# A graph network's second layer: additions, Relu, one-hots and sums of a group moved next to its first products

## The chip, the cores and the metric

The kernel runs on one core of a Trainium2 chip. A core has five engines that run their own programs and wait for each other by semaphores: TensorE (PE, matrix products, with its weight loads PEld), VectorE (DVE), ScalarE (ACT), GpSimd (POOL) and SyncE (SP), which issues most of the DMAs. [...] The metric is the device time of one execution in microseconds (us).

## The reference

The program has 12500 nodes with 64 features and 212500 edges (two random directions of 100000 pairs and a loop at each node), sorted by target. It has two layers, each behind a layer norm and a Relu. The first multiplies each source row by the weight of its edge's relation (16 of them) and sums by target. The second, which the change touches, is a small network on each edge:

```
h = jnp.maximum(_layernorm(x, axis=-1), 0.0)
msg_input = jnp.concatenate([h[src], h[dst], edge_attr], axis=1)
hid = jax.nn.relu(msg_input @ W1 + b1)
msg = hid @ W2 + b2
x = x + jax.ops.segment_sum(msg, dst, num_segments=12500)
```

All in float32.

## The kernel before, in words

The kernel splits W1 by its rows. The first layer ends by writing, for each node, `a_rows` (its row times the part of W1 for sources) and `b_rows` (its row times the part for targets, with b1). An edge's hidden row is then Relu of its source's `a_rows`, plus its target's `b_rows`, plus its eight attributes times the rest of W1. Loop edges are left to a separate path, so some 200000 edges remain. They stand in tiles of 128, four tiles to a group: 391 groups (`NGC`), in the order of their targets, so that one group's targets lie in a window of at most 40 nodes (`W`).

For each group `second_layer` (from line 1382) does this:

- POOL gathers the sources' rows with four indirect DMAs, one a tile, into a landing buffer `rows` (`gather`, line 966). There are 14 such buffers, so POOL can be 14 groups ahead of the addition that empties them.
- SP loads the window of `b_rows` into one of six `b_win` buffers (line 1417), and once in four groups the edges' places in the window (`local_bc`) and their attributes (`of_edges`, lines 1402 to 1412).
- At every second group ACT makes two groups' one-hots by node, with two activations (`off`, then `of_edges`, lines 1428 and 1429).
- **First products:** PE multiplies them with the window into `pz` (line 1435). A float32 product is two matmuls with two weight loads in the trace, so a group has eight of each. The first four groups have more: two further products a tile, for the last blocks of nodes (lines 1436 to 1443). [...]
- **Addition** `z` (line 1448): DVE adds products and gathered rows.
- **Relu** (line 1454): ACT writes `hid`.
- **One-hots** `oh` (line 1456): DVE compares the edges' places with a row of numbers, 128 edges by 40 nodes.
- **Sums** `pa` (line 1470): PE multiplies `hid` by `oh` and so sums the group's edges into 65 by 40. One PSUM tile holds four groups; there are two such tiles.
- **Table addition** (line 1477): DVE adds the 65 by 40 to a running table, `sums`, at a place that it reads from memory into a register.

Beside this, one step an iteration of `open_step` finishes two blocks of nodes in eight groups: it multiplies finished sums by W2 and stores them, and does the loop edges (`results` and `own_edges`, lines 1355 and 1333, whose products all land in `po`).

What sets the order: each engine's instructions are chained in the order in which the Python loop issues them (`InOrder`, line 322, used as `V_`, `S_`, `T_`, `Q_`, `P_`), so the order that is written is the order of every engine's program. The loop at line 1395 runs over iterations `it`; group `it` has its loads, gathers and first products in it, and the other steps of a group come some iterations later. How many is set by four pairs at line 121 and by `turns` (line 127): with a pair `(most, least)` a group's step comes `most` iterations after its first products, and over the last 40 groups the distance shrinks, one in four groups, to `least`. Within an iteration the order is: first products, `z`, Relu and one-hots, sums, one step of `open_step`, table addition. So at iteration `it` PE makes `pz` of group `it` and `pa` of group `it - 6`, DVE makes `z` of `it - 3`, `oh` of `it - 4` and the table addition of `it - 9`.

What an instruction waits for is worked out by the framework from the tiles it touches. [...]

Of the kernel before, what the change touches and what calls it, by code (L numbers as in the profile page):

```python
# [40 lines left out]
F32 = mybir.dt.float32  # L41
# [9 lines left out]
P = 128  # L51
N = 12500
D = 64
# [15 lines left out]
DA = D + 1  # L69


G = 4
W = 40
# [44 lines left out]


L1_PE, L1_ADD = (2, 1), (4, 2)  # L120
L2_Z, L2_HID, L2_PE, L2_ADD = (3, 1), (4, 1), (6, 1), (9, 1)


BEGIN = 8
# [74 lines left out]
def bc(ap, axis, n, shape):  # L199
    return ap.unsqueeze(axis).to_broadcast(shape)  # L200
# [3 lines left out]
def gnn_kernel(  # L204
# [101 lines left out]
    def in_order():  # L306
        with ExitStack() as c2:
# [858 lines left out]
            def chain(*parts):  # L1166
                for part in parts:
                    yield from part
# [147 lines left out]
            def load_mid(k):  # L1316
                b0, nb = BLOCKS[k]
                mids[k] = wk2.tile([P, BS, D], F32, name="x_r", bufs=3)[:, :nb]
                Q_.dma_start(mids[k], x_mid[b0 * P : (b0 + nb) * P, :].rearrange("(b p) d -> p b d", p=P))
# [62 lines left out]
            def second_layer(ps):  # L1382

                iota_p = ps.tile([P, W], F32, name="iota_p", bufs=1)
                V_.tensor_copy(iota_p, iota_s[:, :W])
                for k in range(2):
                    load_mid(k)
                load_own(0)
                open_step = chain(
                    own_edges(0, sums[0], 0, ps), own_edges(BS, sums[0], AHEAD2, ps), own_edges(2 * BS, sums[1], AHEAD2, ps)  # L1390
                )
                a_of, n_of, oh_of, pz_of, hid_of, pa_of = {}, {}, {}, {}, {}, {}
                at, at_b = {}, {}
                of_z, of_hid, of_pe, of_add = (turns(lag, NGC) for lag in (L2_Z, L2_HID, L2_PE, L2_ADD))
                for it in range(NGC + L2_ADD[1]):

                    g = it
                    if g < NGC:
                        if g % RG == 0:
                            at_b.update(enumerate(windows(first_row, g, PAD_DST, Q_, min(RG, NGC - g)), g))  # L1400
                        if g % RB == 0:
                            ng = min(RB, NGC - g)
                            local_bc = wk2.tile([W, RB * G * P], BF16, name="local_bc", bufs=3)
                            Q_.dma_start(
                                local_bc[:, : ng * G * P],
                                dst_l[g : g + ng, :].rearrange("g e -> (g e)").unsqueeze(0).to_broadcast([W, ng * G * P]),
                            )
                            of_edges = wk2.tile([WE, RB * G * P], F32, name="of_edges", bufs=3)
                            Q_.dma_start(
                                of_edges[W:, : ng * G * P].rearrange("c (t e) -> c t e", e=P),  # L1410
                                turned_c[g * G * EA : (g + ng) * G * EA, :].rearrange("(t c) e -> c t e", c=EA),
                            )
                        a_of[g], n_of[g] = gather((a_early if g < EARLY else a_rows)[:, :], src_c, g, NTC)
                        n = n_of[g]
                        if n:
                            bw = b_win[g % NBW]
                            Q_.dma_start(bw[:W, :], b_rows[bass.ds(at_b.pop(g), W), :])
                            if g == 1:
                                for _ in range(2, EARLY):
                                    t = wk2.tile([P, 2, G * P], F32, name="of_last", bufs=EARLY - 2)  # L1420
                                    of_last.append([t[:, k] for k in range(2)])
                                for _ in sources_of_last(range(2, EARLY), wk2):
                                    pass
                            if g % 2 == 0:
                                np_ = min(2, NGC - g)
                                cols = slice(g % RB * G * P, (g % RB + np_) * G * P)
                                off = wk2.tile([W, 2 * G * P], BF16, name="off")[:, : np_ * G * P]
                                S_.activation(off, local_bc[:, cols], AF.Abs, bias=neg_w)
                                S_.activation(of_edges[:W, cols], off, AF.Relu, bias=1.0, scale=-1.0)
                                pz = ps.tile([P, 2, G, D], F32, name="pz", bufs=4)  # L1430
                            pz_of[g] = pz[:, g % 2]
                            for i in range(n):
                                k = (g % RB * G + i) * P
                                more = range(2 if g < EARLY else 0)
                                T_.matmul(pz_of[g][:, i, :], lhsT=of_edges[:, k : k + P], rhs=bw, start=True, stop=not more)
                                for b in more:
                                    T_.matmul(
                                        pz_of[g][:, i, :],
                                        lhsT=of_last[g][b][:, i * P : (i + 1) * P],
                                        rhs=a_last[:, b, :],  # L1440
                                        start=False,
                                        stop=(b == 1),
                                    )
                    for g in of_z.get(it, []):
                        n = n_of[g]
                        if n:
                            hid_of[g] = wk2.tile([P, G, D], F32, name="z", bufs=3)
                            V_.tensor_tensor(hid_of[g][:, :n, :], pz_of.pop(g)[:, :n, :], a_of.pop(g)[:, :n, :], op=ALU.add)
                    for g in of_hid.get(it, []):
                        n = n_of[g]  # L1450
                        if n:
                            z = hid_of[g]
                            hid_of[g] = hid[g % NHID]
                            S_.activation(hid_of[g][:, :n, :D], z[:, :n, :], AF.Relu)
                            oh_of[g] = wk2.tile([P, G, W], F32, name="oh", bufs=5)
                            V_.tensor_tensor(
                                oh_of[g][:, :n, :],
                                bc(local[:, g * G : g * G + n], 2, W, [P, n, W]),
                                bc(iota_p, 1, n, [P, n, W]),
                                op=ALU.is_equal,  # L1460
                            )
                    for g in of_pe.get(it, []):
                        n = n_of[g]
                        if n:
                            if g % 4 == 0:
                                pa = ps.tile([DA, 4, W], F32, name="pa", bufs=2)
                            pa_of[g] = pa[:, g % 4, :]
                            r, o = hid_of.pop(g), oh_of.pop(g)
                            for i in range(n):
                                T_.matmul(pa_of[g], lhsT=r[:, i, :], rhs=o[:, i, :], start=(i == 0), stop=(i == n - 1))  # L1470
                    next(open_step, None)
                    for g in of_add.get(it, []):
                        if n_of[g]:
                            if g % RG == 0:
                                at.update(enumerate(windows(place_row, g, SN + AHEAD2 - W, V_, min(RG, NGC - g)), g))
                            to = sums[STEP[g] % 2][:, bass.ds(at.pop(g), W)]
                            V_.tensor_tensor(to, to, pa_of.pop(g), op=ALU.add)
                        if g in FIN:
                            k = FIN.index(g)
                            for _ in open_step:  # L1480
                                pass
                            if k + 1 < NFIN:
                                n = BLOCKS[k][1] * P
                                V_.tensor_copy(sums[(k + 1) % 2][:, :AHEAD2], sums[k % 2][:, n : n + AHEAD2])
                            open_step = results(k, ps)
                for _ in open_step:
                    pass
# [28 lines left out]
            with tc.tile_pool(name="own_ps2", bufs=1, space=PSUM) as psB:  # L1516
                second_layer(psB)
# [464 lines left out]
```

## Time and profile before

| | us |
|---|---|
| median of three runs | 4862.96 (4859.89 to 4871.01) |
| the profiled execution | 4867.39 |
| its span, first to last instruction | 4865.5 |
| gathers of the second layer | from 2493.4 to the end of the last at 4806 |
| POOL busy, of the span | 2988.6 (61%) |
| PE busy, of the span | 2402.1 (49%) |
| ACT busy | 1615.3 (33%) |
| DVE busy | 1408.1 (29%) |

The profile is one execution, taken by the hardware. A line of a group of instructions names engine, operation, the tile written and those read, their shapes, how often, the busy time, the mean time of one in ns, and then the idle time of the engine just before them with what ended most of it. `issue` means that the engine waited for nothing that the profile shows; `remote` that a wait ended by something that the trace doesn't tie to an instruction. A line of the timeline has the start, the duration, the engine, the instruction, and in brackets the idle time before it. Every instruction here is put down to line 331, the helper through which all are issued, so tiles tell them apart: `pz<-b_win,of_edges` are the first products, `pa<-oh,hid` the sums, `sums<-sums,pa` the table addition. (`pa<-oh_r,rows` and `rows<-h_rows` belong to the first layer.)

### The profile page before, as it was taken

What the parts mean: (1) busy time and instruction counts of PE and PEld (TensorE: products, weight loads), DVE (VectorE), ACT (ScalarE), POOL (GpSimd) and SP (SyncE); (2) the same over time, 40 slices, a digit from 0 to 9 for tenths busy, and PEclk for the clock granted to TensorE, in tenths of its full rate; (3) what the DMA queues carried; (4) which work ended last, traced back from release to release, by engine and by line L of the source; (5) the groups of instructions that cost most, each with busy time, mean ns of one, the idle gap of its engine ahead of it and who ended that gap; (6) DMA issues with size and microseconds to landing.
All of it is one profiled execution on the core that took longest, in us unless ns stands there. A gap on an engine that the chain in (4) does not pass through costs nothing.

```text
span 4865.5 us, 51339 instructions
## 1 busy us (share of the span) xinstructions
PE 2402.1 (49%) x14955; PEld 1987.2 (41%) x14955; DVE 1408.1 (29%) x4923; ACT 1615.3 (33%) x3341; POOL 2988.6 (61%) x3169
## 2 busy tenths in 40 slices
PE   0244434444344444444445565665565656565556
PEld 0123323333233333333335455555555545555456
DVE  5566726355122332322221111111111111111112
ACT  3434434444344444444432222222222222222222
POOL 5366656665566666666655666666666666666663
PEclk9755555555565555555555555555555555555555
DMA  3314231353433311111111111111111111121111
GB/s 96 72 37 83 54 67 39 67 82 58 69 52 55 60 40 38 39 36 35 36 41 35 41 38 40 40 41 40 39 41 39 43 37 42 39 42 39 39 39 28
DMA packets 533688, 230.44 MB, mean 47 GB/s; under 512 B 430834, under 2 KB 472880, under 8 KB 532374
## 3 DMA queue, kind: packets, MB, share of 16 engines
q0 software_dynamic: 101152, 111.42, 12.0%
q1 hardware_dynamic: 418949, 112.45, 11.4%
q10 hardware_dynamic: 13298, 3.20, 0.3%
q8 instruction: 122, 2.00, 0.2%
q14 instruction: 167, 1.37, 0.1%
HBM read 191.53 MB, written 35.25 MB: 47 GB/s over the span
## 4 chain that ended last, share of the span: by engine, by line
PE 20%; another core or an unknown queue 20%; issue 20%; ACT 5%; DVE 3%; POOL 2%; DMA 0%; DVEq 0%; SPq 0%; ACTq 0%; POOLq 0%
PE pz L331 10%; PE pa L331 7%; POOL rows L331 2%; ACT off_r L331 2%; PE po L331 2%; ACT oh_r L331 1%; PE pT L331 1%; DVE table L331 1%; DVE z L331 1%; PE hT L331 1%; ACT off L331 0%; DVE sums L331 0%; DVE oh L331 0%; SPq L331 0%
## 5 line engine op out<-in xcount | busy, mean ns | idle before, releaser
L331 POOL DMA_INDIRECT rows<-h_rows,src_c x1533 | 1458.5, 951 | 875.6 <-issue 400.7
L331 POOL DMA_INDIRECT rows<-a_rows,src_c x1547 | 1463.3, 946 | 830.5 <-issue 425.0
L331 PE MATMUL pz<-b_win,of_edges 48*128 48x64 f32 x3126 | 794.3, 410 | 482.2 <-issue 442.5
L331 PE MATMUL pa<-oh_r,rows 128*64 128x96 f32 x6132 | 705.5, 353 | 603.9 <-issue 412.2
L331 PEld LDWEIGHTS pz<-b_win,of_edges 48*128 48x128 f32 x3126 | 719.7, 320 | 546.5 <-issue 476.4
L331 PEld LDWEIGHTS pa<-oh_r,rows 128*64 128x64 f32 x6132 | 532.9, 208 | 778.6 <-issue 674.6
L331 DVE TENSOR_TENSOR table<-table,pa 128x96 f32 x1565 | 393.9, 252 | 984.8 <-remote 651.0
L331 PE MATMUL pa<-oh,hid 128*65 128x40 f32 x3126 | 468.1, 305 | 337.2 <-issue 317.9
L331 ACT ACTIVATE hid<-z 128x256 f32<-128x256 f32 x391 | 153.4, 405 | 1286.3 <-DVE z L331 1021.3
L331 ACT ACTIVATE off_r<-iota_s,code 128x192 bf16<-128x192 f32 x1535 | 569.3, 443 | 0.0
L331 PEld LDWEIGHTS pa<-oh,hid 128*65 128x65 f32 x3126 | 394.3, 221 | 400.9 <-issue 342.0
L331 ACT ACTIVATE oh_r<-off_r 128x768 f32<-128x768 bf16 x392 | 330.2, 842 | 361.2 <-remote 238.2
L331 DVE TENSOR_TENSOR sums<-sums,pa 65x40 f32 x391 | 73.0, 187 | 1114.2 <-remote 776.0
L331 DVE TENSOR_TENSOR z<-pz,rows 128x256 f32<-128x256 f32 x391 | 163.9, 420 | 312.7 <-issue 248.2
L331 PE MATMUL pT<-table,wrel 128*64 128x256 f32 (+1 forms) x800 | 209.6, 566 | 38.2 <-issue 30.7
L331 ACT ACTIVATE off<-local_bc,neg_w 40x1024 bf16<-40x1024 bf16 x196 | 222.2, 1134 | 17.4 <-DVE z L331 10.7
L331 DVE SCALAR_TENSOR_TENSOR table<-b_rel,rsel,hT 128x256 f32<-128x256 f32 (+1 forms) x400 | 170.5, 468 | 169.2 <-remote 109.0
L331 ACT ACTIVATE of_edges<-off 40x1024 f32<-40x1024 bf16 x196 | 206.7, 1054 | 6.2
L331 PE MATMUL hT<-ident,u_in 128*128 128x128 f32 (+3 forms) x107 | 46.8, 438 | 307.7 <-issue 125.8
L331 DVE COPY_PREDICATED k_a<-move,k_a 128x1712 int32<-128x1712 int32 (+8 forms) x124 | 185.6, 1498 | 2.1 <-DVE move L331 0.2
L331 ACT ACTIVATE hid_l<-o_ab 128x128 f32<-128x128 f32 x49 | 15.1, 308 | 475.9 <-DVE o_ab L331 421.1
L331 PEld LDWEIGHTS hT<-ident,u_in 128*128 128x128 f32 (+3 forms) x107 | 18.3, 171 | 340.8 <-issue 181.1
(242 smaller groups left out, 1614.3 us busy)
## 6 DMA issues: line engine op xcount, KB each, us to landing
rows<-a_rows,src_c POOLq DMA_INDIRECT x1547
rows<-h_rows,src_c POOLq DMA_INDIRECT x1533
local_bc<-dst_l SPq DMA_DIRECT2D x97, 160.0 KB
k_a<-in_attr_k SPq DMA_DIRECT2D x8, 1368.0 KB
k_a<-in_attr SPq DMA_DIRECT2D x4, 1716.0 KB
b_win<-b_rows SPq DMA_DIRECT2D x391, 10.0 KB
u_in<-attr_c SPq DMA_DIRECT2D x97, 64.0 KB
turned_c<-u_out SPq DMA_DIRECT2D x97, 64.0 KB
```

The source lines that it names most:

```text
L331: last_ins[self.engine] = getattr(self.engine, name)(*args, **kw)
```

## The change

```
-L2_Z, L2_HID, L2_PE, L2_ADD = (3, 1), (4, 1), (6, 1), (9, 1)
+L2_Z, L2_HID, L2_PE, L2_ADD = (0, 0), (0, 0), (0, 0), (6, 1)
...
-                                pz = ps.tile([P, 2, G, D], F32, name="pz", bufs=4)
+                                pz = ps.tile([P, 2, G, D], F32, name="pz", bufs=3)
...
-                                pa = ps.tile([DA, 4, W], F32, name="pa", bufs=2)
+                                pa = ps.tile([DA, 4, W], F32, name="pa", bufs=3)
```

At iteration `it` PE now makes `pz` and then `pa` of the same group, DVE makes its `z` and `oh`, ACT its Relu, and the table addition is that of group `it - 6` (nearer at the end). Between `pz` and `pa` of a group nothing else stands in PE's program; the steps of `open_step` follow `pa`. ACT's two activations for a pair of groups stand ahead of the first one's Relu and behind the Relu of the group before. `pz` has three PSUM tiles instead of four, `pa` three instead of two. No instruction is added or left out.

## The prediction

> **What bounds the kernel now.** I read the page's slices and groups first, then the waits in the middle of the second layer (3000 to 4800 us), then the timeline around its pauses and its two ends. The change touches the second layer alone: its gathers run from 2493 us, the last steady ones to 4806, and the span ends at 4865.5. [...]
>
> ```profile
> L331 POOL DMA_INDIRECT rows<-a_rows,src_c x1547 | 1463.3, 946 | 830.5 <-issue 425.0
> L331 PE MATMUL pz<-b_win,of_edges 48*128 48x64 f32 x3126 | 794.3, 410 | 482.2 <-issue 442.5
> L331 PE MATMUL pa<-oh,hid 128*65 128x40 f32 x3126 | 468.1, 305 | 337.2 <-issue 317.9
> ```
>
> The waits of that stretch (engine and tile, what it waited for, us, times, longest):
>
> ```profile
> DVE sums L331 <- remote: 626.2, 37, 20.1
> PE pz L331 <- issue: 347.2, 310, 3.7
> POOL rows L331 <- DVE oh L331: 282.2, 70, 6.4
> ```
>
> DVE stands for up to 20 us at a time, PE loses time with nothing shown that it waits for, and POOL is stopped 70 times. The timeline of one such round (start, duration, engine, instruction, idle time before it):
>
> ```profile
> 3637.48 0.19 DVE L331 TENSOR_TENSOR sums<-sums,pa 65x40 f32 x1 [19.96 <-remote]
> ...
> 3638.38 0.94 POOL L331 DMA_INDIRECT rows<-a_rows,src_c  x1 [3.78 <-DVE oh L331]
> ...
> 3657.13 0.94 POOL L331 DMA_INDIRECT rows<-a_rows,src_c  x1 [0.30 <-issue]
> ...
> 3659.63 0.23 PE L331 MATMUL pa<-oh,hid 128*65 128x40 f32 x1 [0.96 <-issue]
> ...
> 3661.03 0.99 PE L331 MATMUL pa<-oh,hid 128*65 128x40 f32 x7 [1.17 <-issue]
> 3661.05 0.19 DVE L331 TENSOR_TENSOR sums<-sums,pa 65x40 f32 x1 [19.92 <-remote]
> ...
> 3661.95 0.95 POOL L331 DMA_INDIRECT rows<-a_rows,src_c  x1 [3.88 <-DVE oh L331]
> ```
>
> POOL issues 16 gathers (four groups), one every 1.25 us (0.95 and 0.30 of issue), and stops because the 14 landing buffers are full until DVE adds products to rows. PE creeps from 3651 on, one instruction in about 0.7 us, and is free again at 3661.03; in the same moment DVE gets a signal of products that PE had finished long before. That is 22.65 us after the first of 16 gathers. At the layer's start POOL issues 56 gathers (16 of a_early, 40 more) without a full stop:
>
> ```profile
> L331 POOL DMA_INDIRECT rows<-a_early,src_c x16: 942/946/947, 2493.4 to 2512.1; - x16
> ```
> ```profile
> 2564.12 0.94 POOL L331 DMA_INDIRECT rows<-a_rows,src_c  x1 [0.30 <-issue]
> 2571.98 0.29 DVE L331 TENSOR_TENSOR o_ab<-o_ab,po 128x128 f32<-128x128 f32 x1 [43.61 <-remote]
> ```
>
> There the release comes 78.6 us after the first. So (78.6 - 22.65)/(56 - 16) = **1.40 us a gather**, plus 0.27: while gathers follow each other, PE's signals and its issue are held up, until 1.40 us times their number has passed. That is the bound. In the stretch of waits 1217 gathers make 304 groups in 1800 us, 5.92 us a group; 4 x 1.40 = 5.60 of it is this floor, and 70 rounds of 4.34 groups lose (1800 - 1217 x 1.40)/70 = 1.37 us each between release and next gather, 0.32 a group. [...]
>
> **The change part by part.** Nothing is removed or added: as many products, additions, Relus, one-hots and gathers. What changes is what an engine can do ahead.
>
> *Table additions.* Before, the addition of the first of four groups stood where the fourth's products had just been issued in the same accumulator tile, so DVE waited for those and did four groups in one burst. Now it comes six groups after its products, three after the tile's last; DVE should not stand there at all. The 626 us of that wait go, but only DVE loses them, and it is idle anyway. Worth nothing by itself: what is late next is z.
>
> *z, Relu, one-hots and pa without lag.* Now PE may not start pz of the next group before pa of this one, which needs Relu, which needs z, which needs PE's signal for pz. By starts and ends of rows: pz 1.97, 0.1 to z, z 0.42, 0.1, Relu 0.42, 0.05, pa 1.03 to the next pz. At every second group ACT's off and of_edges (1.17 + 1.06) begin only after the Relu before and so stand in the path, instead of beside PE. A pair takes 2.27 + 1.97 + 0.1 + 0.42 + 0.1 + 0.42 + 0.05 + 1.03 + 1.97 + 0.1 + 0.42 + 0.1 + 0.42 = 9.4, with three sets of po products in eight groups (1.03 each, all behind even groups) 10.1: **5.05 us a group** when no signal is held. That is under the floor of 5.60, so by itself it costs nothing; its cover is the floor. But a signal that is held now stops the chain.
>
> *How many groups a round holds.* Count from the first gather. The z that allowed it ended 0.27 before (3661.68, gather 3661.95). Relu ends at 0.25, pa begins at 0.3, the odd group's pz runs from 1.35 to 3.3. Are signals prompt then? The row of o_ab at 3639.80 answers a po that ended at 3639.76, 1.4 us into its round; of the pz that ended 4.9 us into it, at 3643.25, the trace's record of PE's signals has nothing before 3646.9. So the second z comes at 3.4, POOL gets a second buffer before it stops at 5.0, and goes on. Relu to 4.3, off and of_edges to 6.6, pz of the third group to 8.6: that signal is held until 8 x 1.40 + 0.27 = 11.5. Two groups a round. If a round starts with an odd group, the second pz is later by 2.2, and the round may hold one; the next then starts with an even one. The nearest row is in the last 40 groups, where the old lags shrink to one:
>
> ```profile
> 4781.11 0.95 POOL L331 DMA_INDIRECT rows<-a_rows,src_c  x1 [3.90 <-DVE oh L331]
> ...
> 4789.87 0.95 POOL L331 DMA_INDIRECT rows<-a_rows,src_c  x1 [0.30 <-issue]
> ...
> 4792.71 0.42 DVE L331 TENSOR_TENSOR z<-pz,rows 128x256 f32<-128x256 f32 x1 [2.30 <-issue]
> ...
> 4793.41 0.94 POOL L331 DMA_INDIRECT rows<-a_rows,src_c  x1 [2.59 <-DVE oh L331]
> ```
>
> Eight gathers, a round of 12.3 us, 6.15 a group, with the release 11.6 after the first. The loss a round is then 12.3 - 8 x 1.40 = 1.1; bounds: 0.9 (z alone ahead of the gather) and 2.7 (if PE, whose issue is slow too, has part of pz left at the release). I take 1.1 by this row: 5.60 + 1.1/2 = 6.15, **0.23 more than now, times 377 groups behind the first 14, +87 us**.
>
> How much PE has in store decides between 0.9 and 2.7. The row: in the round of 3638 PE issues some 100 instructions at full pace, to 3651, before it creeps. [...] No row of this profile shows which of the two holds for the new order.
>
> *Head.* The first four groups have 24 products of pz each, some 6.6 us, now in line with z, Relu and pa: from the release at 2572 z of group 4 comes about 10 us later than the rows around 2594 show. **+10.**
>
> *Tail.* When the last gather is released, 14 groups are left, at 5.05: 13 x 5.05 + 8 for the last sums and results = 74. Now it is 4865.5 - 4809.3 = 56, at 8.6 a pair. **+18.**
>
> *Buffers and SP.* pz has three PSUM tiles instead of four, pa three instead of two. A pair's z is done two pairs before its tile is wanted again, an addition five groups before: nothing, while the order holds; at worst a wait that the chain already has. SP loads b_win six groups ahead, waiting for pz of six groups before: some 36 us of cover against about 2 of landing. Were it gone, 2 us a group.
>
> Sum: +87 + 10 + 18 = +115 on the profiled execution's own 4867.4: 4982. It stands 4.4 above the median of the runs shown, so 4980 is forecast, about 2.4% slower.
>
> **The rivals.** *Rounds of one, or pairs with PE late.* Speaking for it: signals at 4.9 us are held already. One group a round: 5.60 + 1.1 = 6.70, +0.78 x 377 + 28 = +322, 5190. Pairs at 6.95: +388 + 28, 5283. *Signals stay prompt (faster).* Place: PE's signal for pz to DVE. The hold-up may come from PE's own run-ahead crowding the same path; a PE in step with DVE and ACT sends less at once. For it: in the round from 4757.51 a z at 4764.86 follows its pz (ended 4764.7) at once, 7 us in. Then rounds never end and POOL runs at the floor: 5.60, -0.32 x 377 + 28 = -93, 4770. It decides if the third z of a round comes before POOL has stopped, some 10 us in. Against it: 37 waits of DVE average 17 us. *The new order makes no other rounds than four* (the change does nothing to the bound): +28 alone, 4895. That the order isn't what it says is unlikely: each engine's instructions are chained in the order in which they are written.
>
> **How the numbers follow.** Pairs 0.48 (own range 4940 to 5070, by losses of 0.9 to 1.6 a round); singles or late pairs 0.26 (5100 to 5290); rounds as now 0.08; prompt signals 0.18. The range must reach into both outer cases: 4800 to 5200. Within 0.2% (10 us, about what a measurement of this kernel can tell from no change) is only the stretch between the prompt case and the others: 0.06. Faster 0.17, slower 0.77.
>
> **What would show it.** POOL's stops grow from 70 to about 150 in the same stretch, in rounds of 8 gathers; DVE waits at z, some 5 to 8 us each, not at sums; ACT's off waits for Relu; the floor of 1.40 holds. I am wrong if gathers run on in long rounds (then faster), if POOL stops after every four (singles), or if PE still runs pz when DVE is released (late pairs).

## The result and the profile after

On the chip of the first profile the changed kernel took 4890.78 us (median of five runs, 4889.72 to 4895.72) where the kernel before took 4862.96 (4859.89 to 4871.01): a ratio of 1.0058, interval 1.0045 to 1.007. It is slower, as forecast, but by 28 us and not by 115. The profiled execution took 4890.74, its span is 4888.9, 23.4 more than before.

The same three groups of the page after:

```profile
L331 POOL DMA_INDIRECT rows<-a_rows,src_c x1547 | 1462.7, 945 | 844.1 <-issue 420.9
L331 PE MATMUL pz<-b_win,of_edges 48*128 48x64 f32 x3126 | 771.1, 424 | 236.7 <-issue 166.3
L331 PE MATMUL pa<-oh,hid 128*65 128x40 f32 x3126 | 429.7, 312 | 795.7 <-ACT hid L331 526.7
```

POOL's row is nearly what it was (844.1 us idle, 830.5 before). PE's idle time has moved from `pz` to `pa`: it now stands at the sums of each group until the Relu of the same group is there. The waits of the middle, 3000 to 4800 us:

```profile
DVE z L331 <- issue: 986.8, 202, 9.2
...
POOL rows L331 <- DVE oh L331: 311.1, 163, 3.1
```

DVE stands at `z` and no longer at `sums`. POOL stops 163 times instead of 70, as foretold, but for 1.9 us each and not 4.0, so that the total is only 29 us more in 1800. A round in the timeline:

```profile
3601.10 0.94 POOL L331 DMA_INDIRECT rows<-a_rows,src_c  x1 [3.01 <-DVE oh L331]
...
3605.46 0.42 DVE L331 TENSOR_TENSOR z<-pz,rows 128x256 f32<-128x256 f32 x1 [4.30 <-issue]
...
3609.15 1.96 PE L331 MATMUL pz<-b_win,of_edges 48*128 48x64 f32 x8 [1.67 <-issue]
3609.90 0.95 POOL L331 DMA_INDIRECT rows<-a_rows,src_c  x1 [0.31 <-issue]
...
3611.21 0.42 DVE L331 TENSOR_TENSOR z<-pz,rows 128x256 f32<-128x256 f32 x1 [4.48 <-issue]
...
3611.90 0.95 POOL L331 DMA_INDIRECT rows<-a_rows,src_c  x1 [1.06 <-DVE z L331]
...
3615.65 0.95 POOL L331 DMA_INDIRECT rows<-a_rows,src_c  x1 [0.30 <-issue]
3618.22 0.42 DVE L331 TENSOR_TENSOR z<-pz,rows 128x256 f32<-128x256 f32 x1 [5.96 <-remote]
...
3618.92 0.95 POOL L331 DMA_INDIRECT rows<-a_rows,src_c  x1 [2.32 <-DVE oh L331]
```

The `z` at 3605.46 follows its `pz` (ended 3605.37) at once, 4.4 us into the round, as foretold. The next `pz` ends at 3611.11, ten us into the round, and I had held its signal until 8 x 1.40 + 0.27 = 11.5 us, which is 3612.6. The `z` came at once, at 3611.21; POOL stood still for only 1.06 us, a gather's worth of that count was still left, and the round went on to twelve gathers. Their 12 x 1.40 end at 3618.2, and there the next `z` stands, to 0.1 us.

For all rounds I count 1.4025 us for each gather, from 0.25 us after the start of the round's first one (close to the prediction's 1.40 and 0.27). A round ends when this count has run off before 0.25 us behind the next gather's start, and its loss is the time between the two. Between 2650 and 4780 us:

| | rounds | groups a round | loss a round, us | loss a group | a group, us |
|---|---|---|---|---|---|
| before | 81 | 4.41 | 1.38 | 0.313 | 5.923 |
| after | 153 | 2.34 | 0.79 | 0.337 | 5.947 |

The rounds are half as long and lose a little over half as much each. Behind the last gather the groups go one after the other:

```profile
4861.48 0.42 DVE L331 TENSOR_TENSOR z<-pz,rows 128x256 f32<-128x256 f32 x1 [2.54 <-PE pz L331]
...
4866.40 0.42 DVE L331 TENSOR_TENSOR z<-pz,rows 128x256 f32<-128x256 f32 x1 [2.65 <-PE pz L331]
...
4871.51 0.42 DVE L331 TENSOR_TENSOR z<-pz,rows 128x256 f32<-128x256 f32 x1 [2.85 <-PE pz L331]
```

That is 5.0 us a group. By parts, in the two profiled executions: the second layer starts 3.0 us earlier, the first 100 gathers take 3.1 more, the other 1463 take 9.9 more, and behind the last gather there are 73.0 us instead of 59.6, 13.4 more: together +23.4.

### The profile page after: what moved, and what is told of

It reads as the page before. It is cut to its first block, busy times and chain, and to the rows that moved or that the text cites. A ratio compares the mean times of both kernels' runs of the same rounds, so it can differ in the third digit from the quotient of the medians.

```text
span 4888.9 us, 51576 instructions
## 1 busy us (share of the span) xinstructions
PE 2364.0 (48%) x14955; PEld 1941.0 (40%) x14955; DVE 1417.0 (29%) x4923; ACT 1640.1 (34%) x3341; POOL 2988.4 (61%) x3169
## 5 line engine op out<-in xcount | busy, mean ns | idle before, releaser
L331 POOL DMA_INDIRECT rows<-a_rows,src_c x1547 | 1462.7, 945 | 844.1 <-issue 420.9
L331 PE MATMUL pz<-b_win,of_edges 48*128 48x64 f32 x3126 | 771.1, 424 | 236.7 <-issue 166.3
L331 PE MATMUL pa<-oh,hid 128*65 128x40 f32 x3126 | 429.7, 312 | 795.7 <-ACT hid L331 526.7
L331 PEld LDWEIGHTS pz<-b_win,of_edges 48*128 48x128 f32 x3126 | 695.7, 324 | 298.0 <-issue 202.8
L331 PEld LDWEIGHTS pa<-oh,hid 128*65 128x65 f32 x3126 | 372.9, 226 | 869.3 <-ACT hid L331 528.5
L331 ACT COPY u_out<-hT 128x128 f32<-128x128 f32 (+3 forms) x107 | 27.9, 260 | 296.7 <-remote 163.2
L331 DVE TENSOR_TENSOR oh<-local,iota_p 128x160 f32<-128x160 f32 x391 | 121.0, 310 | 0.0
```

Source lines behind the costliest of these rows:

```text
L331: last_ins[self.engine] = getattr(self.engine, name)(*args, **kw)
```

## The experiments

Two theories stood at the start. **A**, that of the prediction: gathers that follow each other faster than 1.40 us hold PE's signals until the backlog has run off; a round loses the turn from that release to the next gather, and the order of the engines' programs changes rounds and turns. **The rival**: DVE's, PE's or SP's own work, or a path that everything shares, sets 5.9 us a group whatever the order.

The jobs ran on chips that differ. The kernel before took 4860 to 4863 us on those of the result and of runs 5, 6, 11 to 14, 17 and 18 (I call them H), 4902 on that of runs 7 to 10 (H'), and 4034 on those of runs 1 to 4, 15 and 16 (N). Ratios are always to the kernel before on the same chip.

### Chips where nothing is held: runs 1 to 4

Run 1, the kernel before with late additions:

```
-L2_Z, L2_HID, L2_PE, L2_ADD = (3, 1), (4, 1), (6, 1), (9, 1)
+L2_Z, L2_HID, L2_PE, L2_ADD = (3, 1), (4, 1), (6, 1), (12, 3)
...
-                                pz = ps.tile([P, 2, G, D], F32, name="pz", bufs=4)
+                                pz = ps.tile([P, 2, G, D], F32, name="pz", bufs=3)
...
-                                pa = ps.tile([DA, 4, W], F32, name="pa", bufs=2)
+                                pa = ps.tile([DA, 4, W], F32, name="pa", bufs=3)
```

> The kernel before, with only the table additions moved (12 groups behind the first products instead of 9, so 6 behind the sums as in the change) and the change's PSUM tiles (pz 3, pa 3); z, Relu and sums keep their old distances. Theory of held signals (the floor is 1.40 us a gather, and what is lost is the turn from the release of PE's signals to the next gather): before, DVE had four sums to add between release and z, so a round lost 1.37 us; after the change the middle loss was 0.93. With additions late and rounds still of 4 groups: 0.95/4.3 = 0.22 instead of 0.32 a group, -0.10 x 377 = -38, 4825 us. Rival (DVE's wait at the sums is idle time that costs nothing): 4863, within 5. Rival (fewer pz tiles stop PE from running ahead): slower, above 4880.

Run 2, the changed kernel with `L2_ADD = (3, 1)`:

> The changed kernel, with only the table addition nearer again (3 groups behind the sums, as far as before, instead of 6). Theory of held signals: DVE stands at the sums of a finished tile once in four groups, and at a release has up to four additions ahead of z; +0.4 us in about half of the 153 rounds of the middle, some 80 rounds in all of it: +30, 4920 us. Rival (the additions cost nothing wherever they stand): 4891, within 5.

Run 3, the changed kernel with a lag of one over the last 20 groups:

```
-        of.setdefault(max(early(g), g - before + max(least, min(most, most - (g - (n - 40)) // 4))), []).append(g)
+        d = max(least, min(most, most - (g - (n - 40)) // 4)) if most >= least else most if g < n - 20 else least
+        of.setdefault(max(early(g), g - before + d), []).append(g)
...
-L2_Z, L2_HID, L2_PE, L2_ADD = (0, 0), (0, 0), (0, 0), (6, 1)
+L2_Z, L2_HID, L2_PE, L2_ADD = (0, 1), (0, 1), (0, 1), (6, 1)
```

> The changed kernel, with only the last 20 groups' z, Relu and sums one group behind their first products, as in the kernel before. Theory (behind the last gather the time is the chain of pz, z, Relu and sums of one group after the other, 5.05 a group, against 8.6 a pair with one group of lag): the stretch behind the last gather goes from 71 to about 57 us, 4877 us in all. Rival (the tail is set by PE's own products or by the last stores): 4891, unchanged.

Run 4, the changed kernel with a memset behind each gather of the second layer:

```
                         in_offset=bass.IndirectOffsetOnAxis(ap=idx[:, k : k + 1], axis=0),
                     )
+                    if second:
+                        P_.memset(pacer, 0.0)
```

> The changed kernel, with one small memset of 128x4 on GpSimd (0.10 us in the profile) behind every gather of the second layer, so that gathers are issued some 1.35 to 1.42 us apart instead of 1.25. Theory of held signals by a backlog (signals are held only because gathers are issued faster, 1.25, than they are worked off, 1.40): the backlog no longer builds, rounds get long or never end, and a group takes 5.60 to 5.70 instead of 5.94: 4790 us (4770 to 4810). Rival (signals are held whenever gathers follow each other, backlog or not): no gain, 4880 to 4900, or slower by what the memsets take (0.4 us a group: up to 5040).

Measured, beside 4033.63: run 1 4036.10 (1.0006, 0.9997 to 1.0015), run 2 4037.49 (1.0009, 1.0000 to 1.0018), run 3 4054.58 (1.0051, 1.0037 to 1.0065), run 4 4067.59 (1.0083, 1.0069 to 1.0096). The base was 17% lower than I had taken for granted, and none of the four told what it was made for. The timeline of run 3 shows why (its helper is line 332):

```profile
3206.59 1.97 PE L332 MATMUL pz<-b_win,of_edges 48*128 48x64 f32 x8 [1.02 <-ACT of_edges L332]
3207.22 0.94 POOL L332 DMA_INDIRECT rows<-a_rows,src_c  x1 [0.30 <-DMA rows<-a_rows,src_c]
3208.46 0.94 POOL L332 DMA_INDIRECT rows<-a_rows,src_c  x1 [0.31 <-issue]
3208.65 0.42 DVE L332 TENSOR_TENSOR z<-pz,rows 128x256 f32<-128x256 f32 x1 [4.16 <-issue]
```

Here gathers go on at 1.25 us without a stop through the layer, and every `z` comes 0.09 us after its `pz`, though gathers follow each other all the time. So the program alone doesn't make the hold-up; it comes with the chip. (Each chip of these runs served one job, so the chip and what else differed between the jobs can't be told apart.) The chip also measures my chain alone: `z` of groups 20 to 376 stand **5.00 us** a group apart in run 3 (I had worked out 5.05), which is just POOL's 4 x 1.25. And run 4 shows that the memset of 0.12 us nearly hides in the 0.30 between gathers: they came 1.26 apart.

### The pace of the gathers: runs 5, 6, 10 and 11

Run 5 is the changed kernel, run 6 has a memset of 128x208, both on an H chip.

> The changed kernel itself, for a ratio on the chip of this job: on the chip of the first four runs the kernel before took 4033.6 us, gathers went on at 1.25 us each without a stop and no signal was held. If this chip is like that one: the middle is set by POOL's issue (5.00 a group) and, for the changed order, by its chain of 5.00 a group, and only the tail differs: 13 groups at 5.0 behind the last gather's landing less what runs under the gathers; 4050 to 4056, as in the run with the edited tail (4054.6). If it is like the chip of the profiles of before and after: ratio 1.0058, near 4891.

> The changed kernel with a memset of 128x208 on GpSimd behind each gather of the second layer (128x4 took 0.12 us in the run before and set 1.26 between gathers; I expect about 0.30 and 1.44). Where a gather holds PE's signals for 1.40 us of work (the chip of the two profiles): with gathers 1.44 apart no backlog builds, signals come at once, a group takes 4 x 1.44 = 5.76 instead of 5.94, 4820 us; the rival (held as long as gathers follow each other) gives 4890 or more. Where no signal is held (the chip of the first four runs): POOL alone sets the pace, 5.76 instead of 5.00 a group, 391 x 0.76 = +297 on the changed kernel, some 4340.

Measured, beside 4859.77: run 5 4891.31 (1.0066, 1.0053 to 1.008), run 6 4864.74 (1.0009, 1.0000 to 1.0018). The memset took 0.288 us and set 1.40 between most gathers (1.41 on average where POOL didn't stop), not 1.44:

```profile
L331 POOL MEMSET pacer<- 128x208 f32 x1563 | 450.2, 288 | 1.0
```

It gained 27 us on run 5, and of 355 `z` 201 now came at once, some of them 14 us and more into a round. But the others were late, by up to 5 us; POOL stopped once in five to six groups, and a group still took 5.90. At that pace, against 1.4025, A leaves nothing to work off a disturbance with; a rival says that the shared path needs 5.9 a group anyway. Run 10 is the kernel before with the same memset, on H'.

> The kernel before with the memset of 128x208 behind each gather of the second layer, which set 1.41 us between gathers in the changed kernel and let signals come at once up to 14 us into a round. Theory (signals are held by a backlog of gathers, whatever the order of the other engines): rounds get longer here too, the loss a group falls from 0.32 to about 0.1 to 0.25 on a floor of 4 x 1.41 = 5.64: 5.75 to 5.9 a group, 4800 to 4850 us on a chip that holds signals (4860). Rival (the lagged order, with PE running ahead, holds signals by itself): no gain, 4860 or slower. On a chip that holds none: 391 x 4 x 0.16 = +250, 4285.

Measured: 4894.21 beside 4901.90 (0.9981, 0.9972 to 0.9989). There are long rounds now, of eight groups and more, but a group takes 5.93: nearer to the rival than to A, which had forecast 5.9 at most. Run 11 is the changed kernel with 128x256.

> The changed kernel with a memset of 128x256 on GpSimd behind each gather of the second layer, to set about 1.45 between gathers (128x208 set 1.41). Theory A, the one behind the prediction (a gather holds signals for 1.40, and the rest of the 5.94 a group are turns between release and next gather): with 1.45 no backlog ever builds, no signal is held, and a group takes 4 x 1.45 = 5.80: -0.14 x 377 = -54, some 4837 where the changed kernel takes 4891. Rival B (one path serves gathers and the other traffic in turn; a group needs some 5.9 of it, 1.40 a gather when nothing else runs but near 1.475 in the middle, whatever the order): 1.45 is still too fast, signals are held every six to ten groups, and a group takes 5.87 to 5.93: 4862 to 4885.

Measured: 4830.16 beside 4861.47 (0.9925, 0.9913 to 0.9937). The waits of POOL from 3000 to 4800 us:

```profile
POOL rows L331 <- issue: 204.0, 1191, 2.8
POOL rows L331 <- DVE oh L331: 11.7, 12, 1.3
```

311 us of stops have become 12. Gathers come 1.44 apart (1.45 on average), and a group takes 5.84. A had said 4837, the rival 4862 or more. **Slowing POOL down by 0.19 us a gather made the kernel 31 us faster than before the change**, where the changed one took 4891 and 4897 on the other H chips. So no path needs 5.9 us a group whatever the order.

### Gathers, SP's loads and the additions: runs 12 to 14

Run 12 leaves out three of four gathers (`for i in tiles[:1] if second else tiles`, and `z` takes the first tile's rows four times); run 13 is the kernel before with each window loaded a second time, into a spare buffer; run 14 is run 2 again. All on an H chip (4861.47).

> The changed kernel with only the first of a group's four gathers; z adds that tile's rows to all four tiles, so three quarters of the edges get another edge's source row. Both theories: with one gather in five us no signal is held and the chain of pz, z, Relu, sums sets the time, 5.00 a group as on the chip where no signal was held: 391 x 5.00 + 25 = 1980 us behind the start of the second layer near 2490, 4470 us. If instead signals are held by something other than the gathers: 4800 or more.

> The kernel before with each window of b_rows loaded twice, the second time into a spare buffer that nobody reads. Theory A (only gathers hold, SP is idle 90% of the time): unchanged, within 10 us of the kernel before. Rival B (SP's loads are served by the same path as the gathers): each load more takes its share of the 0.3 us a group that are missing between 5.60 and 5.9; with some 1.5 loads a group now, 0.05 to 0.2 more a group, +20 to +80.

> The changed kernel with the table addition 3 groups behind the sums, as near as before, instead of 6, as in the second run, now for a chip that holds signals. Late additions alone made the kernel before 29 us slower, the whole change 29 to 31. If the late additions are what costs (they leave o_ab and the like first in line at DVE while signals are held): back to the kernel before, within 10 us. If the tail of groups one after the other and the other rounds cost (theory A): no better than the changed kernel, 25 to 45 us over the kernel before. On a chip that holds no signals: 4037 beside 4034, as before.

Run 12: 4486.22. From group 20 to 376 the `z` stand 5.00 apart, as on N, and POOL's waits are the mirror of the other runs: it stands idle for DVE after each gather.

```profile
POOL rows L331 <- DVE oh L331: 1102.0, 273, 4.9
```

So the hold-up on H comes with the gathers; without their crowd the same chip gives the same 5.00 as N. Run 13: 4867.37 (1.001, 1.0001 to 1.0018), 6 us for 391 more loads, where the rival had forecast 20 at least: SP's loads have at most a small part in it. (In the profile before SP issues 1556 DMAs and POOL 3148, so SP doesn't issue most of them.) Run 14: 4899.29 (1.0075, 1.0062 to 1.0088), no better than the changed kernel. Near additions lengthen the loss of a round a little (0.96 us, 2.65 groups a round, 5.97 a group): in the order without lag it isn't the late additions that cost.

### Parts of the change where signals are held: runs 7 to 9

All on H' (4901.90). Run 7 leaves out part of the end: with an addition 12 groups late and a loop that runs one iteration past the last group, the table additions of the last two groups and the last block's results aren't issued.

```
-L2_Z, L2_HID, L2_PE, L2_ADD = (3, 1), (4, 1), (6, 1), (9, 1)
+L2_Z, L2_HID, L2_PE, L2_ADD = (6, 1), (7, 1), (9, 1), (12, 1)
...
-                iota_p = ps.tile([P, W], F32, name="iota_p", bufs=1)
+                iota_p = own.tile([P, W], F32, name="iota_p")
...
-                                pz = ps.tile([P, 2, G, D], F32, name="pz", bufs=4)
+                                pz = ps.tile([P, 2, G, D], F32, name="pz", bufs=5)
```

> The kernel before with longer distances: z 6 groups behind the first products instead of 3, Relu 7, sums 9, table additions 12 (each 3 more), five PSUM tiles for pz instead of four, and the one-hots' row of numbers in SBUF, so that the banks suffice. Theory of held signals, on a chip that holds them (kernel before 4860): a release lets DVE do as many groups as PE is ahead, lag plus one, so rounds grow from 4.3 to about 7 groups while a round still loses 1.4 us: 1.4/7 = 0.20 instead of 0.32 a group, -0.12 x 377 = -45, 4815 us. Rival (PE's own issue is held too, and it cannot finish seven groups in a round of 39 us): rounds stay at 4 to 5 and nothing is gained, 4850 to 4870, or PE is late at each release and it is slower, over 4880. On a chip that holds no signals (4034): unchanged within 10, since POOL's issue sets the pace.

Measured: 4945.83 (1.0094, 1.0079 to 1.0109). 73 of its 82 rounds still hold four groups, with 1.72 us of loss. The rival had the right size, but the trace doesn't bear out its reason: when one of DVE's long stands (over 8 us, 3000 to 4750) ended, finished first products were mostly six to eight groups ahead of `z` (two to five in the kernel before), so PE had the groups ready. DVE stood at the table additions:

```profile
DVE sums L331 <- remote: 986.4, 57, 23.3
```

An addition waits for the sums of every group that are issued into its PSUM tile by then: in the tail of the profile after, those of groups 384, 385 and 386 came 0.04 us behind the sums of the next group, and that of 387, the last of its tile, at 4872.08 without a wait. With the old lag the first addition of a tile so waits for the sums of all four groups in it, and this stretch has some 75 such tiles. That these tiles, and not the lag, make rounds of four fits this run and the next; no run changes the number of groups in a tile, so it isn't shown.

Run 8 is run 1 again, run 9 run 3.

> The kernel before with the table additions 12 groups behind the first products instead of 9, and the change's PSUM tiles (pz 3, pa 3), as in the first run, for a chip that holds signals. There: four additions no longer stand between the release and z, so a round of 4.3 groups should lose 0.95 us instead of 1.37: -0.10 x 377 = -38, 4822 us. Rival (DVE's stand at the sums costs nothing): 4860, within 5. On a chip that holds none: 4036 again.

> The changed kernel with the last 20 groups' z, Relu and sums one group behind their first products, as in the third run, for a chip that holds signals. Theory: the 14 groups behind the last gather go at 8.6 a pair instead of 5.0 each (54.7 instead of 62 us for 13 groups, as the run on the other chip had it), and the rounds of the last gathers stay as they are: -7 to -14, 4877 to 4884 us. Rival (the lag makes other rounds under the last 20 groups' gathers, or the tail is the stores): 4891 or slower. On a chip that holds none: 4054 again.

Run 8: 4931.12 (1.0059, 1.0046 to 1.0072). I had forecast a gain of 38 and it lost 29. The release of one of its rounds:

```profile
3608.35 0.29 DVE L331 TENSOR_TENSOR o_ab<-o_ab,po 128x128 f32<-128x128 f32 x1 [10.95 <-remote]
3608.68 0.29 DVE L331 TENSOR_TENSOR o_ab<-o_ab 128x128 f32<-128x128 f32 x1
3608.88 0.19 DVE L331 TENSOR_TENSOR sums<-sums,pa 65x40 f32 x1
3609.04 0.42 DVE L331 TENSOR_TENSOR z<-pz,rows 128x256 f32<-128x256 f32 x1
...
3609.73 0.94 POOL L331 DMA_INDIRECT rows<-a_rows,src_c  x1 [4.15 <-DVE oh L331]
```

In this round DVE doesn't stand at the additions, but it goes on only as far as the next instruction that needs a new signal of PE, here `o_ab`, elsewhere often `oh` (380.6 us in 30 waits, 3000 to 4800); that and what is behind it still come ahead of `z`. ACT's `hid_l` waits for this `o_ab` too (661 us in 37 waits, 3000 to 4800), and behind `hid_l` stand `off` and `of_edges` for PE's next `pz`. Rounds of three and of five groups (43 and 42 of 89) took the place of those of four: 3.99 on average, with 1.59 us of loss, 6.01 a group. The run also has three tiles for `pz` instead of four; PE shows no wait for `z`, which empties them (none in 3000 to 4800). Taking one wait out of a held engine's program moved the stand to the next one.

Run 9: 4929.61 (1.0048, 1.0035 to 1.0061). Behind the last gather it has 61.8 us, run 5 (on an H chip) 72.7: 11 us of the tail are the lockstep of one group after the other.

### The better version: runs 15 to 18

Run 15 is the kernel before with the memset of 128x256 behind each gather of the second layer, run 16 behind each gather of both layers, 17 is 15 again and 18 is the changed kernel again.

> The kernel before with the memset of 128x256 behind each gather of the second layer. In the changed kernel it took POOL's stops away and gave 4830 beside 4861 (0.9925), with a tail of 67 us. Theory A (held signals are a matter of the gathers' pace alone, not of the order of the other engines): the same 5.84 a group, and the old order's tail, 56 to 60: 10 us less, 4820, a ratio of 0.990 to 0.992 on a chip that holds signals. Rival (the lagged order, with PE far ahead, keeps signals held at this pace too, as it did in part at 1.41): 0.996 to 1.00.

> The kernel before with that memset behind each gather of both layers. In the first layer a gather takes 1.51 us on average now (1.25 by POOL's issue, the rest in 184 stops). Theory A: with 1.45 between gathers its stops go as well, up to 0.06 x 1533 = 92 us less, so 4730 to 4790 on a chip that holds signals. Rival (the first layer's stops have other causes, the table additions and ACT's one-hots, or its POOL needs its lead): no gain over the kernel with the second layer alone, or up to 40 slower than that.

> The run before last once more (the old order, a memset of 128x256 behind each gather of the second layer), for a chip that holds signals; the last job ran on one that holds none, where POOL's issue is the bound and the memset made it 1.079 times as long. On a chip that holds signals, theory A (the gathers' pace alone): 5.84 a group and the old tail, a ratio of 0.990 to 0.992. Rival (PE far ahead is held anyway): 0.996 to 1.00. On a chip that holds none: 4352 again.

> The changed kernel, in the same job. On a chip that holds signals (before 4860 or 4900): 1.005 to 1.007 again. On a chip that holds none (before 4034): POOL's issue 5.00 a group in both orders and z of the changed order 40 us behind its gather throughout, because its chain takes 5.00 as well and never makes up for its late start; so only the tail is longer: as the run with the edited tail there (4054.6) and some 7 us more, 4060, a ratio of 1.006 to 1.007.

Runs 15 and 16 fell on an N chip: 4352.37 (1.0788) and 4619.80 (1.145) beside 4033.77, since POOL's issue is the bound there and the memset adds to it (318.6 us for 1563 gathers, 0.20 each, and 586.0 for 3096, 0.19 each). What run 16 was for stays open. Runs 17 and 18 fell on an H chip, beside 4860.78: run 18 4897.45 (1.0070, 1.0057 to 1.0084), run 17 **4778.57 (0.9827, 0.9813 to 0.984)**, the fastest there, and better than A's 0.990. Its profiled execution was its longest, 4803.54. POOL's stops are gone in it as in run 11:

```profile
POOL rows L331 <- DVE sums L331: 7.9, 6, 1.9
POOL rows L331 <- DVE oh L331: 2.2, 3, 1.9
```

The order has a part after all, and in this run the lag is what pays. Without lag a signal is still late at 1.45: in run 11, 201 of 354 `z` came late, by 1.73 us on average and 3.7 at most. In a chain that waits for each signal that makes 5.00 + 1.73 x 201/354 = 5.98 us a group; `z` there stand 5.94 apart, above the gathers' 5.84, and at the end 14 groups are still to be done (68.6 us behind the last gather).

With the old lag signals are late too, and by more. DVE still stands at the additions in run 17:

```profile
DVE sums L331 <- remote: 372.3, 59, 15.1
DVE sums L331 <- PE pz L331: 361.6, 37, 14.4
```

In 64 of 70 tiles DVE stood there for over 2 us (8.9 by the median) when the tile's products had already ended (on N, run 15, 0.6 us at most), though by the count of 1.40 a gather nothing should be held at this pace. So A is wrong that the pace alone decides. The rival, that a PE far ahead keeps signals held, fits, but no run tests it apart. But these stands hardly stop POOL: `z` comes 29 us behind its group's last gather by the median, 74 in the kernel before, so buffers are left. A group takes 5.81, POOL's own pace, and at the last gather 9 groups are still to be done instead of 13, with 41.4 us behind it instead of 59.6. The profiled execution, the slowest of the six, is 64 us below that of the kernel before; the medians are 82 apart, and what the other executions gained more isn't shown.

## Why the prediction was off in size

**The bound held, for rounds that end in a stop.** In the middle of the changed kernel 175 `z` came more than 0.25 us behind their `pz`, and 110 of them within 0.3 us of the end of the count, as the one at 3618.22 above. With three of four gathers left out the time fell by 8%, and at a slower pace POOL's stops vanished. The trace before has the 1.40 once more: near the layer's start, with gathers 1.25 us apart, PE issued one instruction, a weight load or a product, in 1.40 us (in the prediction's round two often come together, which makes its 0.7).

```profile
2543.98 0.29 PEld L331 LDWEIGHTS pz<-a_last,raw_rows 128*128 128x128 f32 x1 [2.52 <-issue]
...
2545.37 0.27 PE L331 MATMUL pz<-a_last,raw_rows 128*128 128x64 f32 x1 [2.52 <-issue]
...
2546.77 0.28 PEld L331 LDWEIGHTS pz<-b_win,of_edges 48*128 48x128 f32 x1 [2.50 <-issue]
...
2548.17 0.26 PE L331 MATMUL pz<-b_win,of_edges 48*128 48x64 f32 x1 [2.53 <-issue]
```

The signals come later than the gathers' data: in the round of the prediction the last gather's packets had ended by 3659.4, no DMA queue moved a packet from then to 3661, and the release came at 3661.03. By the median of all rounds this gap is 1.9 us before and 0.7 after. What kind of path holds them, why N chips don't have it, and what holds signals at 1.44 in the old order (run 17) stays open.

**The step that failed** is how many groups a round holds, and its loss: two groups and 1.1 us, 1.1/2 a group, +0.23 x 377 = +87. The runs showed 2.34 groups and 0.79, 0.337 a group, +0.024 x 377 = +9; that is the 9.9 us of the middle. Two things were wrong in it. I held the third signal until the very end of the backlog; it came when a gather's work was left (44 of the 175 late `z` come with 1.4 to 2.8 us of backlog left, 110 within 0.3 of its end), and with it POOL got a buffer before the round had run off: 74 of 153 rounds have three groups, 57 have two. And where POOL stops for so short a time, little is lost: 38 rounds lose less than 0.5, the others 1.00, near the 1.1 of my row. The row was right for a round with a full stop, but it was one round, in the last 40 groups, where the tail's shorter lags and not the new order made it.

**PE in store.** At the release of 3618.2 PE's held `pz` had been over for two microseconds (begun at 3614.06, 1.97 long), so the case of a PE that is late at each release (2.7 us a round, 6.95 a group) did not come. How much PE has in store no run shows, nor that this decides between 0.9 and 2.7, as I had taken it: the rounds that lost 0.5 or more measured 1.00; two of the 153 lost 2.4, none of the others more than 1.3.

**The chain under the floor** was right: 5.05 forecast, 5.00 in runs 3 and 12. In run 12 POOL waits for DVE, so there the chain itself sets the 5.00.

**Tail** +18: measured +13.4 behind the last gather; by run 9, with a lag of one, lockstep makes some 11 of it.

**Head** +10: measured +3.1. `z` of group 4, which the ten us were for, is 5.9 us later (2600.18, before 2594.24), that of group 8 11 us (2623.58, before 2612.52). But the first `z` comes at 2532.79 instead of 2572.51: it isn't held to the end of the first 56 gathers (some 4 us of the count were left), POOL gets a buffer early and goes on to 60.

**The signs.** POOL's stops: 150 foretold, 163. DVE's waits at `z`: 5 to 8 us foretold, 4.9 on average, 9.2 at the longest. I had ACT's `off` waiting for the Relu; the profile puts under 1 us of wait on `off` in all, since the two stand next to each other and ACT waits at the Relu.

**Table additions** worth nothing: their wait of 626 us went and nothing was won, as said. What I thought after seeing the loss, that four additions ahead of `z` cost 0.4 us a round, gained nothing when they were moved (run 8).

**Buffers and SP** cost nothing, as said: in the profile after PE shows no wait for `b_win` between 3000 and 4800, and a window landed 1.4 us after its issue by the median, where I had taken about 2.

**The rivals.** Prompt signals is what N chips do; POOL then runs at its issue of 1.25 and not at 1.40, which I had not considered. Its reason, that a PE in step with DVE is held less than one that runs ahead, fits runs 11 and 17. "No other rounds than four, +28 alone" gave the right number by luck: rounds halved, the loss a round nearly with them, and tail, head, middle and the earlier start of the layer happened to add up to the same. I had weighed the ways of losing in a round and none in which shorter rounds lose less.

## What to carry to other kernels

If an engine's lead comes in rounds, count what a round loses before multiplying rounds: twice as many stops can cost the same when each is short. Where POOL issues gathers faster than the chip works them off (1.25 us each against 1.40 on H), look at the signals of the other engines before their order; a little more distance between gathers was worth 1.7% here, and a lag under which the stands no longer used up POOL's buffers decided how much of it came through. And measure on more than one chip: the same pace cost 7.9% where nothing was held.

## What the runs showed of the hardware

- One program took 4860, 4902 or 4034 us by the chip, with clocks granted of 0.53 to 0.56 on all. On the last, gathers 1.25 us apart held no signal; on the others rounds that ended in a stop ended 1.40 us a gather after they began, and near the layer's start PE issued one instruction in 1.40 us.
- On the chips that hold, a signal came at once 4.4 us into the round shown, with gathers 1.25 apart, and 14 us and more into some at 1.41. At 1.44 without lag 201 of 354 `z` were late, by 1.73 us on average; at 1.44 with the old lag DVE stood up to 15 us for signals.
- The held signals came 1.9 us after the gathers' last DMA packet in the profile before, 0.7 in the one after (medians of the rounds).
- A memset on POOL of 0.12 us between two gathers moved them by less than 0.01; one of 0.288 by 0.15, one of 0.328 by 0.19 (1.255, 1.401 and 1.441 by the median, 1.25 without).
